# A third sequence's first feed-forward on the experts' lane, and a residual added by TensorE, in a four-stage block of a small model

## The chip, the core and the metric

The kernel runs on one core of one Trainium2 chip. The metric is the device time of one execution in microseconds (us); lower is better. All arithmetic that matters here is in float32.

## The reference

Eight sequences of 512 tokens with 256 features go through six residual steps. Each step first normalises every token (mean and variance, eps 1e-5). Cut to what matters:

```python
x = x + 0.5 * ffn4(ln(x))          # "ffn": gate/up/down with FP4-quantised rows and weights
x = x + retention(ln(x))           # decayed linear attention over the 512 tokens
x = x + 0.5 * ffn4(ln(x))
x = x + 0.5 * mixture(ln(x))       # soft mixture of 8 experts x 128 slots, called "mix 1"
x = x + attention(ln(x))           # 16 heads, causal, LoRA-merged weights
x = x + 0.5 * mixture(ln(x))       # "mix 2"

def ffn4(x):                       # 256 -> 704 -> 256
    h = silu(q(x) @ q(w_gate).T) * (q(x) @ q(w_up).T)
    return q(h) @ q(w_down).T      # q: blocks of 16, scale = max|.|/6, rounded to the FP4 grid

def mixture(x):                    # 1024 slots
    logits = rms(x) @ rms(slot_embeds).T
    slots = softmax(logits, over experts).T @ rms(x)
    processed = gelu(slots @ w1) @ w2
    return softmax(logits, over all slots) @ processed
```

## The kernel before

**Tiling.** A sequence is four tiles of 128 tokens by 256 features and stays in SBUF as `xs[b]` from its load to its store. Weights stay in SBUF throughout. Every matrix product is done in float32 by TensorE into PSUM; the profile shows each float32 product as two records.

**Lanes.** The program is one static instruction stream for each engine, written out ahead of time by a planner. Three `Lane` objects (`front`, `back`, `experts`) each hold a list of units, which are Python generators. A generator yields before each block of TensorE work and says which PSUM banks and which earlier results the block needs. `drive` picks the next block: among the lanes whose block could begin within `SLACK` (0.3 us) of the time that the planner holds for TensorE, it takes the lane with the least `spent`, which is its TensorE time so far, divided by its `SHARE`. Work that is for VectorE and ScalarE alone (quantisation, softmax pieces) goes into chains in `lane.later` and is put where VectorE is free. The planner's own costs stand in `Meter`; they set the order only, not the time on the chip.

**What a feed-forward issues.** For each of its four token tiles: a dozen small VectorE operations for the moments, the normalised rows and the quantisation of the 256 features (with one ScalarE square in between); two transposes (`tr_f`) and a copy back by ScalarE; eight gate and up products (`gu_f`), two ScalarE Silu and two VectorE multiplications; the quantisation of the 704 hidden values (`h_f`: eight VectorE operations with a ScalarE square in between); six transposes (`hTp_f`) and a copy; six down products (`dn_f`); and one VectorE operation that adds half of the PSUM result to `xs[b]`. The last is in `down`, lines 798 to 805. In `retention` the same is done for two tiles at a time (`x<-x,y_r`).

**Order of the sequences.** `front(b)` is the list enter, ffn, retention, ffn, dispatch of mix 1; `back(b)` is enter, attention, dispatch of mix 2. `dispatch` makes the logits (`lt_m`), the softmax over the experts, sends weights through HBM (`ed_m`) and makes the slots (`sl_m`). `experts` is the rest of a mixture: hidden layer (`h_e`), second layer (`p_e`), and the sum over the slots back to the tokens (`mo_e`). Lane `front` starts with sequence 0 and lane `back` with sequence 1 and `BEHIND` (60 us) already on its account. Lane `experts` first runs `other_weights`, which prepares the remaining weights inside the pool `prep`; `drive` returns when that is through, `prep` is freed, and the pool `experts` is allocated (two logits tiles `lg`, two `slT`, two `hid`, one `proc`). From there on the experts' lane has only mixtures in its list, and has nothing to do until sequence 0 has its slots. Sequence 2 is loaded by lane `front` and begins its first feed-forward there, after the dispatch of sequence 0. At most two mixtures are begun and not finished (`room_to_mix`); the list `begun` counts them and the set `mixed` holds those that are through.

The functions that the change touches, and what calls them, with the line numbers of the profile (a helper records every operation, so all of them carry L170 there):

Of the kernel before, what the change touches and what calls it, by code (L numbers as in the profile page):

```python
# [20 lines left out]
FP = mybir.dt.float32  # L21
# [7 lines left out]
P = 128  # L29
# [35 lines left out]
SHARE = {"front": 1.0, "back": 0.9, "experts": 1.15}  # L65

BEHIND = 60.0


class Meter:  # L70
# [178 lines left out]
class Lane:  # L249


    def __init__(self, name):
# [8 lines left out]

        self.places = [0, 1]


class Chain:

# [14 lines left out]
def macaron(ctx: ExitStack, tc: tile.TileContext, a: dict, out: bass.AP):  # L281
# [48 lines left out]

    def wide(lane, name, *shape):

        return shaped(slab.tile([P, 1104], FP, tag=f"wide_{lane.name}", name=name, bufs=WIDE), shape)

    def narrow(lane, name, *shape):

        return shaped(slab.tile([P, 512], FP, tag=f"narrow_{lane.name}", name=name, bufs=NARROW), shape)

    def shaped(t, shape):
        n = int(np.prod(shape))  # L340
# [217 lines left out]
    def quantise_later(lane, v, room, n, name, token, needs=()):  # L558
        def tiles(n, name):
            return [  # L560
                small.tile([P, n], FP, tag=f"{kind}{n}_{lane.name}_{chain.place}", name=f"{kind}_{name}", bufs=1)
                for kind in ("scale", "rec")
            ]

        steps = quantise_steps(v, room, n, name, tiles)
        chain = Chain([(None, step) for step in steps[:-1]] + [(token, steps[-1])], needs, lane.places)
        lane.later.append(chain)
# [66 lines left out]
    def other_weights(lane, prep):  # L634
# [58 lines left out]
        for c0 in (0, 4):  # L693
            yield "p", (("w", "dnq", 0), ("w", "dnq", 1)), ("w", "dn", c0)
            ps = pair(f"dnt_{c0}")
            for c in range(c0, min(c0 + 4, NFC)):
                k = min(P, FF - c * P)
                for d in range(KD):
                    at = ps[:k, c // 2 % 2, (c % 2) * D + d * P : (c % 2) * D + (d + 1) * P]
                    nc.tensor.transpose(at, dn[:, d, c * P : c * P + k], ident)  # L700
            for c in range(c0, min(c0 + 4, NFC)):
                k = min(P, FF - c * P)
                nc.scalar.copy(w_dn[:k, c, :], ps[:k, c // 2 % 2, (c % 2) * D : (c % 2 + 1) * D])


        nc.vector.tensor_reduce(half, hmask.rearrange("p (r u) -> p u r", u=2), AX.X, ALU.add)
# [41 lines left out]

    def ffn(lane, b, tag, after):
        nm = f"f{tag}_{b}"
        y = ys.pop(b)
        yTs, hs, hTs = {}, {}, {}

        def rows_quantised(t):
            needs = [k for k in y["tokens"] if k[2] == t]
            quantise_later(lane, y[t], y["room", t][:, : D // 2], D // QBLK, f"x_{nm}_{t}", ("x", nm, t), needs)  # L760

        def rows_turned(t):
            ps = one(f"tr_{nm}_{t}")
            for d in range(KD):
                nc.tensor.transpose(ps[:, d * P : (d + 1) * P], y[t][:, d * P : (d + 1) * P], ident)
            yTs[t] = y["room", t].rearrange("p (d t) -> p d t", d=KD)
            nc.scalar.copy(yTs[t], ps[:, : KD * P].rearrange("p (d t) -> p d t", d=KD))

        def gate_up(t, f):
            if f == 0:  # L770
                hs[t] = wide(lane, f"h_{nm}_{t}", 3, FH)
            h = hs[t][:, f, :]
            ps = pair(f"gu_{nm}_{t}_{f}")
            for u in range(2):
                for d in range(KD):
                    nc.tensor.matmul(
                        ps[:, u, :FH],
                        yTs[t][:, d, :],
                        w_in[:, d, u * FF + f * FH : u * FF + (f + 1) * FH],
                        start=(d == 0),  # L780
                        stop=(d == KD - 1),
                    )
            nc.scalar.activation(h, ps[:, 0, :FH], AF.Silu)
            nc.vector.tensor_tensor(h, h, ps[:, 1, :FH], ALU.mult)
            if f:
                flat = hs[t].rearrange("p u n -> p (u n)")
                quantise_later(lane, flat[:, :FF], flat[:, FF:], FF // QBLK, f"h_{nm}_{t}", ("h", nm, t))

        def hidden_turned(t):

            h = hs.pop(t).rearrange("p u n -> p (u n)")
            ps = pair(f"hTp_{nm}_{t}")
            for f in range(NFC):
                nc.tensor.transpose(ps[:, f // 4, (f % 4) * P : (f % 4 + 1) * P], h[:, f * P : (f + 1) * P], ident)
            hTs[t] = hT = wide(lane, f"hT_{nm}_{t}", NFC, P)
            nc.scalar.copy(hT, ps.rearrange("p u (c t) -> p (u c) t", c=4)[:, :NFC, :])

        def down(t):
            hT = hTs.pop(t)
            ps = one(f"dn_{nm}_{t}")  # L800
            for f in range(NFC):
                nc.tensor.matmul(ps[:, :D], hT[:, f, :], w_dn[:, f, :], start=(f == 0), stop=(f == NFC - 1))
            xv = xs[b][:, t, :]
            nc.vector.scalar_tensor_tensor(xv, ps[:, :D], 0.5, xv, ALU.mult, ALU.add)
            normalise(lane, b, (t,), after)

        for t in range(2):
            rows_quantised(t)

        for s in range(NT + 3):  # L810
            if s < NT:
                yield "o", (("x", nm, s),), ("T", nm, s)
                rows_turned(s)
                for f in range(2):
                    yield "p", (("T", nm, s),), None
                    gate_up(s, f)
                if s + 2 < NT:
                    rows_quantised(s + 2)
            if 0 <= s - 2 < NT:
                yield "p", (("h", nm, s - 2),), ("H", nm, s - 2)  # L820
                hidden_turned(s - 2)
            if 0 <= s - 3 < NT:
                yield "o", (("H", nm, s - 3), ("w", "dn", 0), ("w", "dn", 4)), None
                down(s - 3)
# [4 lines left out]
    def retention(lane, b, after):  # L829
# [42 lines left out]
        for g in range(NT // 2):  # L872
            yield "o", (("v", nm), ("a", nm, 0), ("a", nm, 1)), None
            ps = one(f"y_{nm}_{g}")
            for i in (2 * g, 2 * g + 1):
                for j in range(i + 1):
                    nc.tensor.matmul(
                        ps[:, (i % 2) * D : (i % 2 + 1) * D],
                        aT[j][:, (i - j) * P : (i - j + 1) * P],
                        v[:, j, :],  # L880
                        start=(j == 0),
                        stop=(j == i),
                    )
            xv = xs[b][:, 2 * g : 2 * g + 2, :]
            nc.vector.tensor_tensor(xv, xv, ps.rearrange("p (c d) -> p c d", c=2), ALU.add)
            normalise(lane, b, (2 * g, 2 * g + 1), after)


# [12 lines left out]
    def dispatch(lane, b, tag, ep):  # L901
# [3 lines left out]
        y = ys.pop(b)  # L905
        yield "p", tuple(y["tokens"]), ("yT", nm)
        yT = columns(lane, y, nm)
        lg = ep.tile([P, NS, S], FP, tag="lg", name=f"lg_{nm}", bufs=2)

        smax = small.tile([P, NS], FP, tag="smax", name=f"smax_{nm}", bufs=2)  # L910
        sums = small.tile([P, NS], FP, tag="sums", name=f"sums_{nm}", bufs=2)
# [118 lines left out]
        def slots(h, d):  # L1030

            ps = one(f"sl_{nm}_{h}_{d}")
            for i in range(NT):
                nc.tensor.matmul(
                    ps,
                    y["all"][:, i, d * P : (d + 1) * P],
                    eds[h, i // 2].rearrange("p (a i n j) -> p i n a j", a=NB, i=2, n=NT)[:, i % 2],
                    start=(i == 0),
                    stop=(i == NT - 1),
                )  # L1040
            if d == 0:
                slTs[h] = ep.tile([P, KD, S], FP, tag="slT", name=f"slT_{nm}_{h}", bufs=2)
            nc.vector.tensor_tensor(slTs[h][:, d, :], ps, rb[h], ALU.mult)


# [9 lines left out]
    def experts(lane, b, tag, ep):  # L1055
        nm = f"e{tag}_{b}"
        slTs, lg = held.pop((b, tag))
        proc = ep.tile([P, NS, W], FP, tag="proc", name=f"proc_{nm}")
        nc.gpsimd.memset(proc[:, :, D:], 2.0)
        for q in range(NQ):  # L1060
            hids = []
            for m in range(NH // 4):
                yield "p", tuple(("slT", b, tag, q // 2, d) for d in range(KD)), ("h", nm, q, m)
                ps = pair(f"h_{nm}_{q}_{m}")
                for c in range(4):
                    for d in range(KD):
# [4 lines left out]
                            start=(d == 0),  # L1071
                            stop=(d == KD - 1),
                        )
                hid = ep.tile([P, 4, QS], FP, tag="hid", name=f"hid_{nm}_{q}_{m}", bufs=HIDS)
                nc.scalar.activation(hid, ps.rearrange("p u (c n) -> p (u c) n", c=2), AF.Gelu)
                hids.append(hid)
            if q == NQ - 1:
# [419 lines left out]
        ]  # L1497

    def room_to_mix():
        return len(begun) < len(mixed) + 2  # L1500

    lanes = [Lane(name) for name in SHARE]
    for lane, b in zip(lanes, range(2)):
        lane.units = front(b)
    lanes[1].spent = BEHIND
    with tc.tile_pool(name="prep", bufs=1) as prep:
        ffn_weights(prep)
        lanes[2].units = [(always, lambda lane: other_weights(lane, prep))]
        drive(lambda: not lanes[2].units and lanes[2].gen is None and not lanes[2].later)
    ep = ctx.enter_context(tc.tile_pool(name="experts", bufs=1))  # L1510
    for b in range(B):
        if b + 2 < B:
            lanes[0].units.append((lambda b=b: b < 2 or (b - 2, 2) in mixed, loading(b + 2)))
            lanes[0].units += front(b + 2)

# [48 lines left out]
```

## Time and profile before

| | |
|---|---|
| time, median of 3 runs | 2965.66 us (2959.52 to 2970.26) |
| profiled execution, its time | 2961.62 us |
| profiled execution, its span | 2959.7 us |
| TensorE matmul (PE) busy | 2812.0 us, 95% of the span |
| TensorE weight loads (PEld) | 1946.7 us, 66% |
| VectorE (DVE) busy | 1651.6 us, 56% |
| ScalarE (ACT) busy | 1174.8 us, 40%, of which 351.5 us in 274 table loads |
| GpSimd (POOL) busy | 128.1 us, 4% |
| mean granted TensorE clock | 0.984 |

The span is from the first to the last instruction on the core; the execution's own time is 1.9 us more. The profile names an operation by the tiles that it writes and reads, with the sequence numbers left out, so `dn_f` stands for the down products of all feed-forwards. "Idle before" is the time that an engine stood still just before these instructions, and the name behind the arrow is what ended it. `PEclk` is the granted TensorE clock as a share of full speed. A matmul's end is modelled, so PE that is busy at a low clock counts as busy.

### The profile page before, as it was taken

The numbers are of one execution on the slowest core, as the hardware profiler recorded it, in microseconds if no ns is written. First come the engines' busy times: TensorE is split into PE (matmuls) and PEld (weight loads), VectorE is DVE, ScalarE is ACT, GpSimd is POOL, SyncE is SP. The second block draws the span as 40 slices with busy tenths as digits, with TensorE's granted clock in tenths as the row PEclk, the third lists the DMA queues.
The fourth block names the chain that finished last, engine by engine and source line by source line (L and its number), as shares of the span: only waits on it lengthen the run. The fifth ranks groups of instructions, "written<-read, shape, count | busy, mean of one in ns | idle before, by whom it ended". The sixth has DMA issues, their size and how long they took to land.

```text
span 2959.7 us, 35020 instructions
## 1 busy us (share of the span) xinstructions
PE 2812.0 (95%) x13550; PEld 1946.7 (66%) x13550; DVE 1651.6 (56%) x4023; ACT 1174.8 (40%) x1587; POOL 128.1 (4%) x232
## 2 busy tenths in 40 slices
PE   4887999999999999999999999999899999999999
PEld 3554777657676577666766667666577666676668
DVE  7676755566565564655647456555565645436340
ACT  3333443434435343343525425254253443443321
POOL 1000000000000000000000000000000000000000
PEclk8988999999999999999999999999999999999999
DMA  3001101020200220002200031000220012000120
GB/s 118 1 0 35 40 24 45 1 75 1 68 1 1 82 64 5 1 1 82 68 1 1 1 114 36 1 1 1 82 68 1 1 43 79 22 1 20 56 75 8
DMA packets 71335, 98.13 MB, mean 33 GB/s; under 512 B 9472, under 2 KB 56320, under 8 KB 71168
## 3 DMA queue, kind: packets, MB, share of 16 engines
q1 hardware_dynamic: 71168, 95.88, 10.8%
q8 instruction: 107, 1.75, 0.2%
q14 instruction: 60, 0.49, 0.1%
HBM read 58.01 MB, written 37.85 MB: 32 GB/s over the span
## 4 chain that ended last, share of the span: by engine, by line
PE 87%; DVE 6%; ACT 4%; issue 1%; DMA 1%; SPq 1%; POOL 0%; ACTq 0%; DVEq 0%; POOLq 0%
PE p_e L170 14%; PE h_e L170 14%; PE gu_f L170 10%; PE lt_m L170 8%; PE sl_m L170 7%; PE mo_e L170 7%; PE dn_f L170 6%; PE s_a L170 4%; PE st_a L170 3%; PE c_a L170 2%; PE qk_a L170 2%; ACT L170 1%; PE hTp_f L170 1%; PE a_r L170 1%; PE y_r L170 1%; PE k_r L170 1%
## 5 line engine op out<-in xcount | busy, mean ns | idle before, releaser
L170 PE MATMUL h_e<-slT_m,w1g 128*128 128x256 f32 x2048 | 464.9, 381 | 4.2 <-DVE lg_m L170 2.4
L170 PE MATMUL p_e<-w,hid_e 128*128 128x256 f32 x2048 | 456.1, 381 | 3.4 <-ACT hid_e L170 2.0
L170 PEld LDWEIGHTS p_e<-w,hid_e 128*128 128x128 f32 x2048 | 386.3, 190 | 70.6 <-issue 13.3
L170 PEld LDWEIGHTS h_e<-slT_m,w1g 128*128 128x128 f32 x2048 | 382.3, 190 | 74.6 <-issue 11.2
L170 ACT ACT_TABLE_LOAD x274 | 351.5, 1283 | 109.0 <-DVE st_a L170 41.3
L170 PE MATMUL gu_f<-w_in,y_ffn 128*128 128x352 f32 x1024 | 333.8, 478 | 13.3 <-ACT y_ffn L170 11.8
L170 PEld LDWEIGHTS gu_f<-w_in,y_ffn 128*128 128x128 f32 x1024 | 198.7, 197 | 131.3 <-issue 19.4
L170 DVE TENSOR_REDUCE nmx<-s_a 128x2 f32<-128x256 f32 (+3 forms) x256 | 195.9, 818 | 126.3 <-PE s_a L170 126.1
L170 ACT ACTIVATE pT_a<-st_a 128x1024 f32<-128x1024 f32 (+1 forms) x192 | 159.0, 878 | 217.9 <-DVE st_a L170 205.1
L170 PE MATMUL lt_m<-yT_m,seT 128*128 128x512 f32 x512 | 235.5, 607 | 4.1 <-ACT yT_m L170 3.6
L170 ACT ACTIVATE hid_e<-h_e 128x1024 f32<-128x1024 f32 x128 | 130.8, 1023 | 268.5 <-PE h_e L170 268.1
L170 PE MATMUL mo_e<-proc_e,lg_m 128*128 128x257 f32 x1024 | 233.3, 381 | 2.9 <-DVE x L170 1.7
L170 PE MATMUL sl_m<-ed_m,y_dis 128*128 128x512 f32 x512 | 227.1, 594 | 3.9 <-DVE lg_m L170 3.3
L170 PEld LDWEIGHTS mo_e<-proc_e,lg_m 128*128 128x128 f32 x1024 | 190.7, 190 | 39.5 <-issue 4.9
L170 ACT COPY proc_e<-p_e 128x512 f32<-128x512 f32 x64 | 37.5, 586 | 391.9 <-PE p_e L170 391.9
L170 DVE TENSOR_SCALAR_CACHE_REDUCE lg_m<-lt_m 128x512 f32<-128x512 f32 x128 | 84.8, 682 | 173.3 <-PE lt_m L170 173.3
L170 PE MATMUL dn_f<-w_dn,hT_f 128*128 128x256 f32 x768 | 177.3, 383 | 0.0
L170 PEld LDWEIGHTS sl_m<-ed_m,y_dis 128*128 128x128 f32 x512 | 95.9, 190 | 114.9 <-issue 106.7
L170 PEld LDWEIGHTS lt_m<-yT_m,seT 128*128 128x128 f32 x512 | 96.2, 194 | 114.4 <-issue 101.3
L170 DVE TENSOR_TENSOR h_f<-h_f,gu_f 128x352 f32<-128x352 f32 x128 | 66.4, 519 | 177.8 <-ACT h_f L170 177.1
L170 PEld LDWEIGHTS dn_f<-w_dn,hT_f 128*128 128x128 f32 x768 | 143.1, 192 | 23.0 <-issue 4.2
L170 DVE TENSOR_TENSOR st_a<-st_a,causalT 128x256 f32<-128x256 f32 x256 | 100.9, 428 | 100.4 <-PE st_a L170 97.7
(197 smaller groups left out, 3246.3 us busy)
## 6 DMA issues: line engine op xcount, KB each, us to landing
d_ed_m<-ed_m SPq DMA_DIRECT2D x256, 128.0 KB
ed_m<-d_ed_m SPq DMA_DIRECT2D x64, 512.0 KB
rb_m<-row_rb_m SPq DMA_DIRECT2D x32, 256.0 KB
x<-in_L_attn_x SPq DMA_DIRECT2D x8, 512.0 KB
tm_m<-row_nm_m SPq DMA_DIRECT2D x16, 256.0 KB
out<-x SPq DMA_DIRECT2D x8, 512.0 KB
row_rb_m<-z_rb_m SPq DMA_DIRECT2D x128, 0.5 KB
w1g<-in_L_ffn_w SPq DMA_DIRECT2D x1, 1024.0 KB
```

The source lines that it names most:

```text
L170: call(*args, **kwargs)
```

## The change

The experts' lane gets one more unit ahead of its mixtures. When `other_weights` is through, a pool `mix` is opened for the first logits tile and `slT`, and behind it a temporary pool `early` with the wide and narrow tiles of a third lane (four narrow tiles where the other lanes have six). In it the experts' lane loads sequence 2, enters it and runs its first feed-forward, with an account that starts `AFTER` (40 us) above that of lane `back`. When that feed-forward is written out, `early` is freed and the second logits tile, `hid` and `proc` take its place; until then the second dispatch may not begin (`room_to_mix`), nor the first `experts`. Lane `front` then has for sequence 2 only an enter for the retention and what follows.

Second, the residual. The factor 0.5 moves into `w_dn`. As long as `mixed` is empty when a block is written out, `down` and `retention` add `x` inside the PSUM accumulation by one more product, identity times `x`, for each tile (`plus`), and ScalarE copies the sum back into `x` (`onto`). After the first mixture, VectorE adds the PSUM result to `x` as before.

```diff
+AFTER = 40.0
...
+        self.slabs, self.narrow, self.held = None, NARROW, None
...
     def wide(lane, name, *shape):
-        return shaped(slab.tile([P, 1104], FP, tag=f"wide_{lane.name}", name=name, bufs=WIDE), shape)
+        return shaped(lane.slabs.tile([P, 1104], FP, tag=f"wide_{lane.name}", name=name, bufs=WIDE), shape)
     def narrow(lane, name, *shape):
-        return shaped(slab.tile([P, 512], FP, tag=f"narrow_{lane.name}", name=name, bufs=NARROW), shape)
+        return shaped(lane.slabs.tile([P, 512], FP, tag=f"narrow_{lane.name}", name=name, bufs=lane.narrow), shape)
...
-                nc.scalar.copy(w_dn[:k, c, :], ps[:k, c // 2 % 2, (c % 2) * D : (c % 2 + 1) * D])
+                nc.scalar.activation(
+                    w_dn[:k, c, :], ps[:k, c // 2 % 2, (c % 2) * D : (c % 2 + 1) * D], AF.Copy, scale=0.5
+                )
...
+    def plus(x, ps):
+        if not mixed:
+            nc.tensor.matmul(ps, ident, x, start=False, stop=True)
+
+    def onto(x, ps):
+        if mixed:
+            nc.vector.tensor_tensor(x, x, ps, ALU.add)
+        else:
+            nc.scalar.copy(x, ps)
...
             for f in range(NFC):
-                nc.tensor.matmul(ps[:, :D], hT[:, f, :], w_dn[:, f, :], start=(f == 0), stop=(f == NFC - 1))
-            xv = xs[b][:, t, :]
-            nc.vector.scalar_tensor_tensor(xv, ps[:, :D], 0.5, xv, ALU.mult, ALU.add)
-            normalise(lane, b, (t,), after)
+                nc.tensor.matmul(
+                    ps[:, :D], hT[:, f, :], w_dn[:, f, :], start=(f == 0), stop=bool(mixed) and f == NFC - 1
+                )
+            plus(xs[b][:, t, :], ps[:, :D])
+            onto(xs[b][:, t, :], ps[:, :D])
+            if after:
+                normalise(lane, b, (t,), after)
...
-                        stop=(j == i),
+                        stop=bool(mixed) and j == i,
                     )
-            xv = xs[b][:, 2 * g : 2 * g + 2, :]
-            nc.vector.tensor_tensor(xv, xv, ps.rearrange("p (c d) -> p c d", c=2), ALU.add)
+                plus(xs[b][:, i, :], ps[:, (i % 2) * D : (i % 2 + 1) * D])
+            onto(xs[b][:, 2 * g : 2 * g + 2, :], ps.rearrange("p (c d) -> p c d", c=2))
...
     def room_to_mix():
-        return len(begun) < len(mixed) + 2
+        return len(begun) < len(mixed) + 2 and f"lg{len(begun) % 2}" in ep
...
+    ep["lg0"] = ep["slT"] = ctx.enter_context(tc.tile_pool(name="mix", bufs=1))
+
+    with tc.tile_pool(name="early", bufs=1) as early:
+        lanes[2].slabs, lanes[2].held, lanes[2].narrow = early, early, NT
+        lanes[2].spent = lanes[1].spent + AFTER
+        lanes[2].units = [
+            (always, loading(2)),
+            (always, lambda lane: enter(lane, 2, "ffn")),
+            (always, lambda lane: ffn(lane, 2, 0, None)),
+        ]
+        drive(lambda: not lanes[2].units and lanes[2].gen is None and not lanes[2].later)
+    ep["lg1"] = ep["hid"] = ep["proc"] = ctx.enter_context(tc.tile_pool(name="experts", bufs=1))
     for b in range(B):
-        if b + 2 < B:
+        if b == 0:
+            lanes[0].units += [(always, lambda lane: enter(lane, 2, "retention"))] + front(2)[2:]
+        elif b + 2 < B:
             lanes[0].units.append((lambda b=b: b < 2 or (b - 2, 2) in mixed, loading(b + 2)))
             lanes[0].units += front(b + 2)
```

The remaining lines of the diff give the tiles of `dispatch` and `experts` the pool that holds them (`ep["slT"]`, `ep["hid"]`, `ep["proc"]`, `ep["lg0"]` and `ep["lg1"]` in turn) and the quantisation's small tiles the pool `lane.held`.

More of the change, by code (lines that the diff above doesn't have):

```diff
@@ L560, in tiles @@
             return [
-                small.tile([P, n], FP, tag=f"{kind}{n}_{lane.name}_{chain.place}", name=f"{kind}_{name}", bufs=1)
+                lane.held.tile([P, n], FP, tag=f"{kind}{n}_{lane.name}_{chain.place}", name=f"{kind}_{name}", bufs=1)
                 for kind in ("scale", "rec")
@@ L907, in dispatch @@
         yT = columns(lane, y, nm)
-        lg = ep.tile([P, NS, S], FP, tag="lg", name=f"lg_{nm}", bufs=2)
+        lg = ep[f"lg{begun.index((b, tag)) % 2}"].tile([P, NS, S], FP, tag="lg", name=f"lg_{nm}")
         smax = small.tile([P, NS], FP, tag="smax", name=f"smax_{nm}", bufs=2)
@@ L1041, in slots @@
             if d == 0:
-                slTs[h] = ep.tile([P, KD, S], FP, tag="slT", name=f"slT_{nm}_{h}", bufs=2)
+                slTs[h] = ep["slT"].tile([P, KD, S], FP, tag="slT", name=f"slT_{nm}_{h}", bufs=2)
             nc.vector.tensor_tensor(slTs[h][:, d, :], ps, rb[h], ALU.mult)
@@ L1057, in experts @@
         slTs, lg = held.pop((b, tag))
-        proc = ep.tile([P, NS, W], FP, tag="proc", name=f"proc_{nm}")
+        proc = ep["proc"].tile([P, NS, W], FP, tag="proc", name=f"proc_{nm}")
         nc.gpsimd.memset(proc[:, :, D:], 2.0)
@@ L1073, in experts @@
                         )
-                hid = ep.tile([P, 4, QS], FP, tag="hid", name=f"hid_{nm}_{q}_{m}", bufs=HIDS)
+                hid = ep["hid"].tile([P, 4, QS], FP, tag="hid", name=f"hid_{nm}_{q}_{m}", bufs=HIDS)
                 nc.scalar.activation(hid, ps.rearrange("p u (c n) -> p (u c) n", c=2), AF.Gelu)
@@ L1499, in room_to_mix @@
     def room_to_mix():
-        return len(begun) < len(mixed) + 2
+        return len(begun) < len(mixed) + 2 and f"lg{len(begun) % 2}" in ep
+    ep = {}
     lanes = [Lane(name) for name in SHARE]
     for lane, b in zip(lanes, range(2)):
+        lane.slabs, lane.held = slab, small
         lane.units = front(b)
@@ L1507, in macaron @@
         ffn_weights(prep)
+        lanes[2].held = prep
         lanes[2].units = [(always, lambda lane: other_weights(lane, prep))]
         drive(lambda: not lanes[2].units and lanes[2].gen is None and not lanes[2].later)
-    ep = ctx.enter_context(tc.tile_pool(name="experts", bufs=1))
+    ep["lg0"] = ep["slT"] = ctx.enter_context(tc.tile_pool(name="mix", bufs=1))
[9 more added lines that the diff above has]
+    ep["lg1"] = ep["hid"] = ep["proc"] = ctx.enter_context(tc.tile_pool(name="experts", bufs=1))
     for b in range(B):
-        if b + 2 < B:
+        if b == 0:
+            lanes[0].units += [(always, lambda lane: enter(lane, 2, "retention"))] + front(2)[2:]
+        elif b + 2 < B:
             lanes[0].units.append((lambda b=b: b < 2 or (b - 2, 2) in mixed, loading(b + 2)))
```

## The prediction

> **What bounds the kernel now.** I read the page first, for who is busy and where it is not.
>
> ```profile
> PE 2812.0 (95%) x13550; PEld 1946.7 (66%) x13550; DVE 1651.6 (56%) x4023; ACT 1174.8 (40%) x1587; POOL 128.1 (4%) x232
> ...
> PE   4887999999999999999999999999899999999999
> DVE  7676755566565564655647456555565645436340
> ...
> PEclk8988999999999999999999999999999999999999
> ```
>
> PE is the bound, and its holes are in the first four slices of 74 us, where DVE is busiest. So I cut the span where the work changes: the experts' lane ends its weights at 75 us, the first `h_e` runs at 317 us, and the first mixture is through at 485 us. The columns are PE, PEld, DVE, ACT, POOL busy, granted clock, DMA share, GB/s.
>
> ```profile
> 0.00:75.00 75.00, 36.84 (x101) 24.21 (x102) 54.46 (x117) 26.90 (x57) 8.19 (x20) 0.88 0.37 117
> 75.00:317.00 242.00, 198.79 (x701) 127.59 (x700) 169.09 (x415) 75.53 (x125) 13.24 (x22) 0.88 0.08 23
> 317.00:485.00 168.00, 168.00 (x703) 126.37 (x702) 99.54 (x256) 71.03 (x95) 10.03 (x18) 1.00 0.11 30
> 485.00:2959.70 2474.70, 2408.37 (x12050) 1668.51 (x12048) 1328.49 (x3238) 1001.36 (x1311) 96.60 (x172) 1.00 0.11 32
> ```
>
> From 317 us on a mixture fills PE whenever the others can't. Before, only lanes `front` and `back` have work: PE is idle for 242 - 198.8 = 43.2 us and the clock is 0.88. The waits of PE in 75 to 317 us (total, times, longest) say for whom:
>
> ```profile
> PE tr_f L170 <- DVE scale_h_f L170: 17.7, 2, 13.9
> PE tr_f L170 <- DVE y_ffn L170: 6.8, 1, 6.8
> PE gu_f L170 <- ACT y_ffn L170: 5.0, 8, 1.7
> PE tr_m L170 <- DVE y_dis L170: 4.8, 2, 3.5
> PE tr_r L170 <- DVE y_ret L170: 4.2, 4, 1.9
> ```
>
> Nearly all end on quantisation or normalisation. The chain (start, us, what) shows what a hole costs besides:
>
> ```profile
> 160.24 8.05 PE gu_f L170 x16
> 170.16 5.00 PE gu_f L170 x16
> 175.82 2.59 PE dn_f L170 x12
> ...
> 198.00 6.66 PE k_r L170 x8
> ...
> 430.79 3.43 PE k_r L170 x8
> ```
>
> The sixteen `gu_f` behind the 6.8 us hole at 152 us take 8.05 us, sixteen undisturbed ones 5.00; eight `k_r` 6.66 and 3.43. Eight such groups in 75 to 317 us sum to 18.2 us over their undisturbed times (1.6 + 0.3 + 1.7 + 2.9 + 3.0 + 3.2 + 3.1 + 2.4). So the stretch holds 198.8 - 18.2 = 180.6 us of PE work at full clock, and loses 61.4 of its 242 us. That is the purse of this change.
>
> **Part one, the moved feed-forward.** On PE, from undisturbed groups: eight `gu_f` blocks at 2.37 us, four `dn_f` at 2.59, four `hTp_f` at 0.66, four `tr_f` at 0.22: 18.9 + 10.4 + 2.6 + 0.9 = 32.8 us. This now lies behind 317 us, where PE is full, and leaves that place entirely. On DVE, by the rows of 75 to 317 us: a tile's rows cost 0.41 + 0.18 + 0.09 + 0.41 for the normalisation and 0.41 + 0.17 + 0.25 + 0.17 + 0.42 + 2 x 0.42 + 0.42 for the quantisation, 3.77 us; its hidden values 2 x 0.52 + 0.88 + 0.18 + 0.43 + 0.19 + 0.89 + 2 x 0.89 + 0.89, 6.26 us. Four tiles: 40.1 us, the residual left out. On ACT 3.3 us a tile, 13.2 us.
>
> Its load is one DMA of 512 KB, moved from 307 us to about 75 us. On SP's queue and on the DMA engines nothing lies between 75 and 275 us (DMA share 0.00), so it delays nobody; at the 175 GB/s of the first 50 us it takes about 3 us (an estimate), covered by the 40 us that this lane stands behind the others. Its first tile must wait for the last readers of `prep`, the `se` transposes that end at 79 us: covered alike. The two pairs of `power` on POOL (0.8 us each) are nothing to an engine that is 5% busy. The enter for the retention normalises sequence 2 anew in front of `tr_r`; the same operations ran behind `down` before, and at that place a mixture covers PE. The second `lg`, `hid` and `proc` wait for the feed-forward's end: the second dispatch first writes `lg` at 407 us, 90 us of room; `hid` is needed at the first `h_e`, and that is the wait to fear (below).
>
> **Part two, the residual.** A product of identity and 256 columns costs one sixth of the `dn_f` group, 0.43 us. Until the first mixture is through there are 24 before the first `h_e` (12 tiles of the three feed-forwards in the stretch, 4 of the moved one, 8 of two retentions): 10.4 us; and 12 after it (last 4 of sequence 1, retention and second feed-forward of sequence 2): 5.2 us, in a full PE, a plain loss. DVE loses 12 x 0.422 + 4 x 0.684 = 7.8 us in the stretch. ACT gains 16 x 0.37 (as `y_ffn<-tr_f`, 128x256 from PSUM) and, for the retentions, 4 x 0.59 (as `proc_e<-p_e`), 8.3 us. The wait for `dn_f` and `y_r`, 8.5 us of idle DVE in these rows, goes to ACT, where the next Silu, square or copy of either lane queues behind it; with ACT at 75.5 + 13.2 + 8.3 = 97 us of 242, I cost that at nothing, at most at the same 8.5 us. The 0.5 in `w_dn` replaces a copy by a copy.
>
> **The sum.** Let T be the time from 75 us to the first `h_e`; it was 242. Gain = 32.8 - 5.2 - (T - 242) = 269.6 - T. PE needs 180.6 + 32.8 + 10.4 = 223.8 us, DVE 169.1 + 40.1 - 7.8 = 201.4 us. So DVE, not PE, is the scarcer of the two by what it reached so far: its share was 169.1/242 = 0.70. The ends: it stays at 0.70, T = 288; or PE is packed at 0.98, T = 228, with DVE at 0.88. That last share is no fancy, 275 to 325 us has it (43.99 of 50 us). A third lane gives both engines something to do while the others wait, but a planner with three DVE-hungry lanes won't hold the best 50 us for 250. I take the middle, 0.79: T = 255, PE at 0.88. **Gain 269.6 - 255 = 14.6 us.** On the profiled execution, 2961.6 - 14.6 = 2947.0; the median stands 4.0 us above it, so 2951. The change breaks even at a DVE share of 0.747. About 0.3%, 8.9 us, is what a measurement of this kernel can tell from no change: a share of 0.772.
>
> The Trainium skill has a rule that speaks against part two: Perfetto Trace Analysis, Identifying the Most-Contended Engine, says to find the engine with the highest occupancy and improve that one first; PE has 95% here, and the change loads it to relieve an engine at 56%. By that rule the products are a loss, 15.6 us of PE time for nothing. The same page, Optimization Strategy, adds that the most contended engine can change from regime to regime; the row of 75 to 317 us, with PE waiting for DVE, is such a regime, and I side with the row.
>
> **The rivals.**
>
> *The identity products cost in full* (the rule above): PE, not DVE, sets T, so relieving DVE saves nothing. Without part two DVE would need 209.2 us, T = 265 at 0.79; part two is worth 10 - 5 = 5 us in my sum, and -15.6 here: 14.6 - 4.8 - 15.6 = -6 us, 2971. For it: PE at 0.88 is not far from full. Against: the waits end on DVE.
>
> *DVE can't do it* (the slower one). DVE's share stays at 0.70, the feed-forward is not through when sequence 0 has its slots, and the first `h_e`, the one filler, waits for it: T = 288, 18 us slower, 2984. It decides from a share below 0.747. For it: the average with two lanes was 0.70 with the planner filling DVE's holes too, and lane `front` shares DVE with a third lane. Against: of DVE's 72.9 idle us in the stretch, 39 end on ACT's Silu or square of `h_f`, which is just where another lane's chain fits.
>
> *All fits*: PE at 0.98, gain 269.6 - 228 = 41 us, 2925. Against: 275 to 293 us, where lane `front` is in its dispatch; if the moved work is used up by then, that hole of 13.9 us stays.
>
> *The gain is given back later*. Everything after 485 us is planned anew; PE has 66 us of idle time there. At 2846 to 2868 us a `p_e` and `mo_e` of the last mixture but one cover the softmax and the DMAs of the last; if the new order leaves these 21 us bare, 14.6 - 21 = -6 us, 2972.
>
> *The lane doesn't get its turns*. 40 us behind on the account, it runs only in holes; half of it (16 us) is left at the first slots and is then done with PE at 0.75, which loses 5 us; 16.4 - 15.6 - 5 = -4 us, 2970.
>
> **Chances.** Forecast (share 0.75 to 0.84) 0.50, of which 0.40 lies beyond 8.9 us; all fits 0.10; DVE can't 0.15 (0.13 beyond 8.9 us, 0.02 within); products in full 0.10; given back 0.08 (half within, half beyond); no turns 0.07. Faster 0.40 + 0.10 = 0.50; slower 0.13 + 0.04 = 0.17; the same 0.33. The range goes from 2928, close to a full packing, to 2979, a DVE share of 0.71; outside are the far ends of the two extreme cases, and of the late one. The forecast's own range is 2936 to 2965 (shares 0.84 and 0.75).
>
> **What would show it.** Right: in 75 to 330 us DVE busy near 0.79, PE idle under 30 us, clock above 0.93; `x<-in_L_attn_x` of sequence 2 near 75 us; the moved feed-forward's last `dn_f` before the first `sl_m`; the first `h_e` near 330 us; about 36 pairs of records of identity products, each 0.43 us. Wrong: a first `h_e` beyond 345 us; PE waiting there for `hid` or the end of the moved lane; a `dn_f`-to-`x` wait on ACT behind table loads; or an early stretch as forecast with more than 66 us of PE idle time behind it.

## The result, and the profile after

The changed kernel takes 2957.62 us (median of 17 runs, 2956.00 to 2961.24) against 2964.26 us (17 runs, 2959.52 to 2970.26): ratio 0.9978, 95% interval 0.9971 to 0.9986. It is 6.6 us faster, 0.22%: clear of noise in that many runs, but below the 0.3% that I had set as a change, and less than half of the 14.6 us that I forecast. The profiled executions are closer together than the medians: 2961.62 us before, which is 2.6 under that kernel's median, and 2958.17 us after. So the profiles below show about half of the gain.

The page of the changed kernel (busy time and share of each engine, then the 40 slices of 74 us):

```profile
PE 2824.4 (96%) x13620; PEld 1962.0 (66%) x13620; DVE 1639.7 (55%) x3992; ACT 1189.9 (40%) x1620; POOL 127.4 (4%) x230
...
PE   4889899999999999999999999999899999999999
...
DVE  7787637446565464655646456555565655436340
...
PEclk8999899999999999999999999999999999999999
```

TensorE has 70 records more, 35 products, and the hole of the fourth slice is gone. A new one shows in the fifth slice. The windows, cut at the first `h_e`, which now comes at 342.5 us (columns as before: PE, PEld, DVE, ACT, POOL, clock, DMA share, GB/s):

```profile
0.00:75.00 75.00, 35.95 (x101) 24.15 (x102) 54.54 (x118) 26.97 (x58) 8.21 (x20) 0.83 0.41 124
75.00:342.50 267.50, 237.57 (x902) 160.85 (x901) 200.83 (x486) 106.34 (x181) 14.18 (x24) 0.95 0.06 19
...
342.50:2956.40 2613.90, 2550.93 (x12621) 1776.97 (x12619) 1384.34 (x3390) 1056.62 (x1384) 105.01 (x186) 0.99 0.11 32
```

From 75 us to the first `h_e` it is T = 267.5 us, 25.5 more than before; everything behind it is 2613.9 instead of 2642.7 us, 28.8 less. VectorE's work in the stretch is 200.83 us, so its share is 0.75. TensorE's idle time there fell from 43.2 to 29.9 us, and the clock rose from 0.88 to 0.95. What TensorE still waits for (total, times, longest):

```profile
PE tr_f L172 <- DVE y_ffn L172: 11.2, 4, 4.8
PE gu_f L172 <- ACT y_ffn L172: 5.9, 11, 0.7
PE nm_m L172 <- DVE top_m L172: 4.3, 1, 4.3
PE tr_f L172 <- DVE scale_h_f L172: 3.8, 1, 3.8
```

The 13.9 us wait is gone; many short ones remain. Where they lie, by the rows of TensorE in order of time (start, duration, operation, idle before):

```profile
282.97 2.75 PE L172 MATMUL dn_f<-w_dn,hT_f 128*128 128x256 f32 x12
285.56 0.59 PE L172 MATMUL dn_f<-x,ident 128*128 128x256 f32 x2
...
299.57 1.11 PE L172 MATMUL nm_m<-ident,top_m 128*128 128x128 f32 x4 [4.26 <-DVE top_m L172]
...
308.71 7.11 PE L172 MATMUL sl_m<-ed_m,y_dis 128*128 128x512 f32 x16 [0.43 <-DMA ed_m<-d_ed_m]
317.71 0.44 PE L172 MATMUL tr_f<-ident,y_ffn 128*128 128x128 f32 x2 [1.90 <-DVE y_ffn L172]
...
329.51 0.66 PE L172 MATMUL tr_f<-ident,y_ffn 128*128 128x128 f32 x2 [3.53 <-DVE y_ffn L172]
...
335.53 7.13 PE L172 MATMUL sl_m<-ed_m,y_dis 128*128 128x512 f32 x16
342.50 3.62 PE L172 MATMUL h_e<-slT_m,w1g 128*128 128x256 f32 x16
```

The `dn_f` pair at 283 and 286 us is the last of the moved feed-forward. From there to 342.5 us TensorE has only sequence 1's second feed-forward beside the dispatch of sequence 0, and 12 of the 29.9 idle us lie there. The two halves of the slots are 27 us apart. Before, they came back to back:

```profile
302.98 13.90 PE L170 MATMUL sl_m<-ed_m,y_dis 128*128 128x512 f32 x32
```

### The profile page after: what moved, and what is told of

Its sections match the earlier page's. It is cut to its first block, busy times and chain, and to the rows that moved or that the text cites. A ratio compares the mean times of both kernels' runs of the same rounds, so it can differ in the third digit from the quotient of the medians.

```text
span 2956.4 us, 35162 instructions
## 1 busy us (share of the span) xinstructions
PE 2824.4 (96%) x13620; PEld 1962.0 (66%) x13620; DVE 1639.7 (55%) x3992; ACT 1189.9 (40%) x1620; POOL 127.4 (4%) x230
## 4 chain that ended last, share of the span: by engine, by line
PE 88%; DVE 5%; ACT 4%; issue 1%; SPq 1%; DMA 1%; POOL 0%; ACTq 0%; DVEq 0%; POOLq 0%
PE p_e L172 15%; PE h_e L172 14%; PE gu_f L172 10%; PE lt_m L172 7%; PE sl_m L172 7%; PE mo_e L172 7%; PE dn_f L172 6%; PE s_a L172 4%; PE st_a L172 3%; PE c_a L172 2%; PE qk_a L172 1%; PE y_r L172 1%; ACT L172 1%; PE hTp_f L172 1%; PE a_r L172 1%
```

## The experiments

The kernels were run in two groups, each on one chip with its own runs of the kernel before (medians 2964.69 us for e1 to e4, 2965.12 us for e5 to e8). The changed kernel's 2957.62 us comes from a third group (2964.26 us), so a difference to it can be off by 0.9 us on that account alone. Gains and losses below are differences of medians, unless the text says otherwise. The question was which of the two parts falls short, and by what mechanism.

### Each part alone

**Part one alone (e1)**: `plus` and `onto` as they are after the first mixture, from the start. The `stop` flags of the products before them are set to match.

```diff
-        if not mixed:
+        if not True:
             nc.tensor.matmul(ps, ident, x, start=False, stop=True)
...
-        if mixed:
+        if True:
             nc.vector.tensor_tensor(x, x, ps, ALU.add)
...
```

> Part one alone: the third sequence's feed-forward stays on the experts' lane, the residual is added by VectorE throughout (no identity product). Theory A (VectorE sets the stretch from 75 us to the first h_e, so the products pay for themselves): VectorE needs 7.8 us more there; at the share of 0.75 that the changed kernel reached, T grows from 267.5 to about 278 us, less 4.8 us for the 11 products behind it: about 2963, no gain over the kernel before. Theory B (the products lie on TensorE's path in full): 35 products of 0.43 us, 15 us, are given back: about 2943.

Measured: 2950.50 us, ratio to before 0.9959 (0.9946 to 0.9973): 14.2 us faster than before by the medians, 12.2 by the ratio, which is 0.41% (8.0 to 16.0). Two of its six runs, at 2956.7 us, lie among those of the changed kernel; the other four are at 2949 to 2951. Theory A, which is my prediction's, had 2963, theory B 2943; half of what the products cost by B comes back. Part one alone is better than the whole change by 7.1 us (5.6 by the ratios), so part two is a loss.

The first `h_e` comes at 329.8 us, but T can't be compared with that of the changed kernel: less work lies in it. The `gu_f` records from 75 us to the first `h_e`, of the changed kernel and of this one:

```profile
L172 PE MATMUL gu_f<-w_in,y_ffn 128*128 128x352 f32 x287 | 99.8, 503 | 5.9 <-ACT y_ffn L172 5.9
L172 PE MATMUL gu_f<-w_in,y_ffn 128*128 128x352 f32 x262 | 88.9, 493 | 4.6 <-ACT y_ffn L172 4.6
```

The 25 records that are missing, of sequence 1's second feed-forward, come behind the first `h_e` here.

**Part two alone (e2)**: the kernel before with identity products (no pool `early`, `front(2)` whole in lane `front`).

> Part two alone: the residual by identity products until the first mixture is through, no moved feed-forward. Theory A: VectorE loses 7.8 us of 169.1 in 75 to 317 us, T falls by about 8 to 11 us, 5 us are lost behind it: about 2959. Theory B: TensorE's work grows by 15 us, of which what falls into holes costs nothing: between the time of before and 15 us more, 2964 to 2979.

Measured: 2967.89 us, ratio 1.0013 (1.0003 to 1.0023): 3.2 us slower. The first `h_e` comes at 314.3 us, 2.7 us earlier, and everything behind it takes 2652.4 us, 9.7 more. Some 3.6 us of that are the two profiled executions' (the one of the kernel before lies 3.1 under the median of this group, this one 0.6 above), so about 6 remain. So the early stretch gains a little with two lanes, less than the 8 to 11 us that I expected, and what lies behind it, with 12 products of 0.43 us and another order, takes more back.

**Products only until the slots (e3)**: `slotted` in place of `mixed` in the conditions of `plus` and `onto`.

> The whole change, but identity products only until sequence 0 has its slots (23 or 24 instead of 35). Nothing before the first h_e changes. Both theories: 11 or 12 products of 0.43 us leave a full TensorE, 4.8 us less than the whole change, about 2953. If what is written out behind the slots comes out in another order with another sum of holes, it is off from that by as much; so this run also gives the size of what re-planning alone does.

Measured: 2951.29 us, ratio 0.9957 (0.9944 to 0.9970), 6.3 us below the whole change, where 4.8 were expected. The first `h_e` comes at 343.2 us; up to there the instructions are those of the changed kernel, so the two T, 268.2 and 267.5 us, show how closely T repeats. The remainder is 2605.3 us. The products behind the slots are a plain loss of about the size costed; the 1.5 us more may be the new order's, which this run doesn't separate. The time is also that of part one alone within 0.8 us: the 24 products before the first `h_e` and the relief of VectorE there gain nothing together, as far as two kernels with different orders can be compared.

### One suspected cost at a time, with the order held

For the next three, the planner was charged for an instruction as in the changed kernel, and another one, or none, was issued in its place. So every other instruction of each engine kept its place. The helper `planned` charges the planner for the engine and operation that it is given by name, and issues the call behind them.

**No products (e5).** The sum leaves out `x`; the `stop` flags of the products before are set to match.

```diff
-            nc.tensor.matmul(ps, ident, x, start=False, stop=True)
+            planned("PE", "matmul", lambda *a, **k: None, ps, ident, x)
...
```

> The whole change with every other instruction in its place, but the 35 identity products are not issued, so x is lost from the sum there (ScalarE still copies). Theory B (all on TensorE's path): 35 x 0.43 = 15 us less than the whole change, about 2942.5. Theory A (only the 11 behind the slots lie on the path, the other 24 in holes): 4.8 us less, about 2953. What lies between tells how many of the 24 cost.

Measured: 2943.94 us, ratio 0.9923 (0.9909 to 0.9937): 13.7 us below the whole change, of 15.1 us that 35 products take. Windows of this kernel, to and from its first `h_e`:

```profile
75.00:331.80 256.80, 226.88 (x854) 151.36 (x854) 200.79 (x486) 107.08 (x181) 14.18 (x24) 0.95 0.07 20
...
331.80:2939.40 2607.60, 2544.69 (x12599) 1772.33 (x12597) 1384.17 (x3390) 1056.63 (x1384) 104.00 (x186) 0.99 0.11 32
```

VectorE has the same work (200.79 us), and T is 10.7 us shorter: 24 products of 0.43 us are 10.4 us. TensorE was idle for 30 us of that stretch, and still the products in it cost their full length. (Behind the first `h_e` the two profiled executions differ by 6.3 us, for 11 products of 4.7 us; the medians leave 3.0 for it.)

**The copy on VectorE (e6).**

```diff
-            nc.scalar.copy(x, ps)
+            planned("ACT", "copy", tc.nc.vector.tensor_copy, x, ps)
```

> The whole change with every instruction in its place, but the copy of x + result out of PSUM is done by VectorE instead of ScalarE, at the same place. Theory D (ScalarE, which in the changed kernel stood 46 us waiting for dn_f and y_r with Silu, squares and copies queued behind, is the price of part two): 5 to 10 us less than the whole change, 2948 to 2953. Rival (the price is the products' TensorE time): no change within 2 us, or slower by up to the 11 us that 29 copies of about 0.4 us take on VectorE.

Measured: 2965.53 us, ratio 1.0000 (0.9991 to 1.0008): 7.9 us slower than the whole change, and no faster than the kernel before. ScalarE's waits in the changed kernel and the copies' rows on VectorE in this one (up to the first `h_e` of each):

```profile
ACT x L172 <- PE dn_f L172: 33.2, 16, 2.6
ACT x L172 <- PE y_r L172: 12.8, 4, 4.8
```

```profile
L172 DVE COPY x<-dn_f 128x256 f32<-128x256 f32 x16 | 6.8, 423 | 21.1 <-PE dn_f L172 21.1
L172 DVE COPY x<-y_r 128x512 f32<-128x512 f32 x4 | 2.8, 692 | 5.2 <-PE y_r L172 5.2
```

```profile
75.00:352.70 277.70, 242.84 (x902) 162.08 (x901) 208.03 (x506) 99.60 (x161) 13.67 (x24) 0.94 0.06 19
```

Twenty copies, 9.6 us of VectorE by their rows, and the first `h_e` comes at 352.7 us, 10.2 us later. VectorE's busy time grew by less, from 200.8 to 208.0 us, and the copies stood 26.3 us at the head of its queue. So in this order ScalarE is the better place for the copies, by 7.9 us, and theory D, which expected a gain, falls. The run doesn't show that the 46 us in which ScalarE stood cost nothing, because the standing moved to VectorE together with the work.

**No Silu beside the dispatch (e7).**

```diff
-            nc.scalar.activation(h, ps[:, 0, :FH], AF.Silu)
+            if (b, tag) == (1, 2):
+                planned("ACT", "activation", lambda o, i, f: tc.nc.scalar.activation(o, i, AF.Copy), h, ps[:, 0, :FH], AF.Silu)
+            else:
+                nc.scalar.activation(h, ps[:, 0, :FH], AF.Silu)
```

> The whole change with every instruction in its place, but the eight Silu of sequence 1's second feed-forward, which run beside the Exp of the first dispatch, are plain copies: Silu is left out there, and with it the table loads around. Theory E (ScalarE's table loads set how long the dispatch of sequence 0 takes, 269 to 342 us, and so T): first h_e 8 to 13 us earlier, the time 6 to 12 us lower, 2946 to 2952. Rival (VectorE sets it): under 2 us.

Measured: 2953.89 us, ratio 0.9959 (0.9945 to 0.9973), 3.7 us below the whole change; first `h_e` at 339.0 us, 3.5 us earlier. The table loads from 75 us to the first `h_e` fell from 18 to 8, which is 12.8 us of ScalarE. Less than a third of that reaches the end. That lies between the theories: the loads are a part of what sets the dispatch, and not the whole. My prediction has no term for them, though the changed kernel has twice as many as part one alone (first row the changed kernel, second part one alone):

```profile
L172 ACT ACT_TABLE_LOAD x18 | 23.1, 1283 | 0.3
L172 ACT ACT_TABLE_LOAD x9 | 11.5, 1283 | 0.1
```

So some of the 7.1 us between these two may be table loads that the other order brings; no run separates them.

### When the moved lane gets its turns

Part one alone with `AFTER` 60 (e4) and 55 (e8; the same line with 55.0):

```diff
-AFTER = 40.0
+AFTER = 60.0
```

> Part one alone with AFTER 60 instead of 40: the moved lane is held back longer, so more of its work should be left for the hole in the first dispatch (295 to 335 us in the changed kernel), where the moved lane has nothing more to do. Theory C (the moved work is used up too early): TensorE idle in the dispatch of sequence 0 shrinks by 5 to 10 us and the time is as much below part one alone. Rival (VectorE, or ScalarE with its table loads, is what the dispatch waits for): same T as part one alone within 3 us.

> Part one alone with AFTER 55. Theory C (holding the lane back leaves work for the dispatch): between AFTER 40 (2950.5) and 60 (2945.7), about 2947. Rival (these differences are what re-planning the rest of the order happens to give): anywhere within some 8 us of those, with the early stretch the same within 3 us.

Measured: 2945.71 us, ratio 0.9937 (0.9923 to 0.9952), and 2943.75 us, ratio 0.9922 (0.9908 to 0.9936). The two windows to and from the first `h_e`, of part one alone with `AFTER` 40 and then with 55:

```profile
75.00:329.80 254.80, 219.78 (x819) 147.25 (x818) 193.19 (x476) 79.31 (x138) 14.77 (x23) 0.94 0.07 20
...
329.80:2947.30 2617.50, 2553.20 (x12633) 1777.66 (x12631) 1402.63 (x3428) 1062.76 (x1389) 104.80 (x187) 0.99 0.11 32
```

```profile
75.00:329.70 254.70, 220.86 (x822) 146.66 (x821) 193.93 (x480) 78.52 (x138) 14.29 (x23) 0.94 0.06 20
...
329.70:2941.50 2611.80, 2558.49 (x12632) 1780.97 (x12630) 1400.90 (x3426) 1076.80 (x1398) 104.68 (x187) 0.99 0.11 32
```

The early stretch is the same: 254.8 and 254.7 us, TensorE idle for 35.0 and 33.8. (With 60 it is 256.6 and 35.7; that profiled execution took 2951.36 us, 5.7 above its kernel's median, so only its early stretch is used.) Theory C falls: the time goes down by 5 to 7 us, but not because TensorE stands less in the stretch, where its idle time changes by 1.2 us at most. The 5.7 us between 40 and 55 lie behind the first `h_e`, where the two kernels have the same instructions in another order. With `AFTER` 40 and with 55 the moved lane's last `dn_f` comes after the slots, at about 327 us, and the first `h_e` waits for it. From the end of the slots to the first `h_e`, with `AFTER` 40 and then with 55:

```profile
314.00:329.80 15.80, 15.80 (x66) 11.50 (x65) 13.29 (x25) 5.48 (x10) 0.00 (x0) 1.00 0.00 0
298.30:329.70 31.40, 28.04 (x124) 20.66 (x123) 27.18 (x52) 8.45 (x16) 0.00 (x0) 1.00 0.00 1
```

TensorE is busy for 15.8 of 15.8 and for 28.0 of 31.4 us, so the wait that I feared costs little there.

Part one alone with `AFTER` 55 beats both kernels: 21 us below the kernel before, about 14 below the changed one.

## Why the prediction was right or wrong

**What bounds the kernel** was right: the holes before the first `h_e`, and the clock behind them. With part one alone TensorE's idle time there fell from 43.2 to 35.0 us and the clock rose from 0.88 to 0.94.

**The frame of the sum** held. Gain = 269.6 - T gives 2.1 us for T = 267.5 (2.5 with 35 products instead of 36), and the spans of the two profiled executions differ by 3.3 us; the rest of the 6.6 us between the medians is these two executions' distance from their medians. Behind the first `h_e` I expected 27.6 us less and 28.8 came. VectorE's work in the stretch, 201.4 us by the rows, was 200.8.

**Part one** came out near its size. Without part two, at the share of 0.79, the rivals' paragraph has T = 265, hence 10 us; measured 14.2 (8.0 to 16.0 by the ratio). That is in part luck: VectorE's share in e1 is 193.2/254.8 = 0.76, not 0.79, and with the 209.2 us of VectorE work that I had there it would give T = 275 and no gain. The first `h_e` came before that work was done, and the rest ran behind it.

**Part two is the term that was mis-sized**, and with it the step to T. I charged the products with 5.2 us, those behind the slots, because VectorE was the scarcer engine and TensorE had holes, and credited the relief of VectorE with some 10 us: +5 in all. Measured with the order held, the products cost 13.7 us (10.7 us of T in the profiles), and the copy on ScalarE instead of VectorE is worth 7.9: together 5.8 us lost. The two parts' comparison (2957.62 against 2950.50) says 7.1, and 6.3 of them go when the products behind the slots are left out. So those cost about what I had charged, and the some 10 us of relief in the stretch did not come: the products there, which I had put into TensorE's holes at no charge, took it. Thus 14.2 us of gain became 6.6.

**The failing inference** is "T is VectorE's demand over a share". It lets work on the other engine go free. The runs show that in this stretch 10.4 us on TensorE made T 10.7 us longer, and 9.6 us of copies on VectorE 10.2, while the changed kernel has the two engines idle there for 30 and 67 us. So TensorE's idle time was no room for the products; that is shown, with the order held and T repeating within 0.7 us. For VectorE it is not as clear, because the copies both worked and waited there. That the two engines alternate as links of one chain is my reading of these two numbers. The signs that I had named did not catch this: TensorE's idle time, 29.9 us, and the clock, 0.95, came as I had written for the case that I was right, with TensorE 10.4 us busier by the products themselves; the first `h_e`, at 342.5 instead of near 330 us, and VectorE's share told.

**The rivals.** "The identity products cost in full" was right on its mechanism, by e5; its time, 2971, was too high, since its base was my share and not the 14.2 us. The rule of the Trainium skill (Perfetto Trace Analysis, Identifying the Most-Contended Engine: improve the engine with the highest occupancy first, and judge TensorE's headroom by MFU, its share of peak arithmetic, or by the busy share of its weight loads) came out right for the products: TensorE leads VectorE's 56% by its weight loads (66%) as by its matmuls (95%), and it was the wrong place for 15 us more, even in the stretch where it waited for VectorE. I had sided with the row against it. "VectorE can't do it" came half true: its share was 0.75, at the break-even, but the moved feed-forward was through at 286 us, well ahead of the slots. In e1 and e8 it was not, and there the wait is filled. The hole that I named against "all fits" is the one that stayed: it moved from 275 to 293 us to 286 to 342 us. "Given back later" didn't happen here, but e4 and e8 show that another order can be worth 5 to 7 us. "The lane doesn't get its turns" didn't happen in the changed kernel, whose moved feed-forward was done early. Whether the copies' wait on ScalarE cost nothing, as I had put it, stays open.

## What to carry to other kernels

Where the waits suggest that two engines take turns, don't count the idle time of one as room: here 10.4 us of products put beside 30 us of idle time cost 10.7 us. Cost work that is moved between two such engines at its full length on both sides, and compare 0.43 us on TensorE with 0.42 us on VectorE before calling it a relief. Compare two times up to a mark only if the same work lies before the mark. A change of two parts should be costed, and run, part by part; here one part won 12 to 14 us and the other lost 6 to 7, and a forecast of the sum hid it. In a program whose order a planner writes, hold the order when a single cost is to be measured, since a changed constant alone moved the time by 7 us.

## What the runs showed of the hardware that I had not expected

ScalarE stood for 46 us with a copy at its head, waiting for TensorE, and was still the better place for it: putting the same copies at the same places on VectorE was 7.9 us slower. And ten table loads of 1.28 us fewer before the first `h_e`, nearly all of them in the 73 us of the dispatch in which ScalarE was busy for 35.6, moved the end by 3.7 us, not by 12.8.
